# A hybrid attention and SSD block on one core: a softplus series on another engine, one joined run of half matmuls, filler matmuls, and a new order

## The chip, the core and the metric

The kernel runs on one core of a Trainium2 chip. The core has five engines that work side by side, each with its own in-order queue of instructions: PE (TensorE, matrix products; its weight loads are shown apart as PEld), DVE (VectorE), ACT (ScalarE), POOL (GpSimd) and SP (SyncE, which issues DMAs here). Data lie in SBUF; PE writes to PSUM, which has eight banks. The metric is the device time of one execution in microseconds, the median of several executions. Before the change it is 804.33 us (three runs: 802.57, 804.33, 809.08).

## What is computed

The input `x` holds 32 sequences of 256 tokens with 128 features, f32. Four sublayers follow, each as `x = x + f(layernorm(x))`:

```python
x = x + attn_a(layernorm(x))     # gated delta rule: a scan over time, done in blocks
x = x + ffn(layernorm(x))        # silu(x wg) * (x wu) wd, hidden size 384
x = x + attn_b(layernorm(x))     # SSD (a state space layer): 4 heads of 64, chunks of 32
x = x + ffn(layernorm(x))        # the same weights
```

The change lies in `attn_b`. Its core:

```python
xBC = silu(causal_conv4(xBC))                 # x, B, C
dt = softplus(dt + dt_bias)                   # one number per token and head
dA_cs = cumsum(dt * A)                        # within a chunk
y_diag = (C B^T * exp(dA_cs_i - dA_cs_j), lower triangle) @ (x * dt)
y_off = exp(dA_cs) * (C @ carried state)
y = (y_diag + y_off + x * D) * silu(z)
out = (y * rsqrt(mean(y*y) + eps) * norm_w) @ W_out
```

## The kernel before

Two sequences (512 tokens, four tiles of 128) make a unit; there are 16 units, each going through all four sublayers. The kernel does not issue instructions as it builds them. `units()` records every operation of all units in a `Planner` (`pl`): its engine, an assumed busy time, an assumed latency, what it reads and writes. Then `run()` writes one order for the whole program. It takes, again and again, the operation that can start first; among those within 20 ns of it, the one with the smallest key. The key is the unit's nominal time (`at`: 17.9 us per unit plus the unit's entry of `SHIFT`; `LAST` shortens the distance of the last units) plus how far the operation is from the end of its unit's longest path. `HOP` is the time that a result is assumed to need to another engine, `SLACK` the time before a buffer can be used again. `SWITCH` is the handicap of an ACT operation that needs another function table, `KEEP` that of a PE operation that changes between full and half tile (`cut`), and `CUT` the time which that change is assumed to take. Operations given to `batch` are placed directly one after another on PE. At the end the operations are emitted in order of planned start, so each engine's queue is fixed when the program is built; on the chip, semaphores hold each instruction until its inputs are there.

PSUM is handed out in eight slots (kind "ps"); a planned buffer is bound to a bank when its first operation is placed.

The parts that the change touches:

- In `ssd`, lines 1010 to 1033: `z` is dt before the softplus, [128 x 16] for a unit. softplus(z) = max(z, 0) + log(1 + e), with e = exp(-|z|), made on ACT. The log is a series: p = 1/(2 + e), r = 2 e p, then a polynomial in r squared by five steps, times r. All of it runs on DVE (`vec`): two instructions for p, one for r, one for the square, one for the first term, five for the polynomial, one for the product with r, one for `dt`. Then POOL makes `dA = dt * A`.
- What follows from `dA`: `pe` and `ee` (PE, ACT), `grid` (three DVE instructions), `cs` (PE), `cut` (four DVE instructions), and six DMAs on SP (three `cuts`, one `sums_s`, two `sums_t`). `dt` itself is read by `xd` (POOL) and `f0` (DVE).
- Lines 1097 to 1178, a loop over the unit's two sequences. For each: transposes of x, `xd`, the products C B^T (`cb_ps`), the decays (`pl` on PE, Exp on ACT, `sm` on DVE), then `py` (shown as sy_ps_s in the profile): 16 products for y_diag as one batch, each two instructions, all with 64 columns of weights; then y, the carried part (`pf`, `yo`), the gate `gz`, the mean square, and the output projection (`so`).
- `power_half` on POOL (two instructions) gives every 1/sqrt: four layer norms per unit (`rstd`) and the SSD's own (`rs`).
- In the profile, L238 is `matmul`, L251 `transpose`, L259 and L261 ACT operations, L275 `vec`, L292 `pool`, L302 a DMA issue. Names end in the sublayer: _a attention, _f first FFN, _s SSD, _h second FFN.

Of the kernel before, what the change touches and what calls it, by code (L numbers as in the profile page):

```python
# [15 lines left out]
ALU = mybir.AluOpType  # L16
AX = mybir.AxisListType

P = 128
# [128 lines left out]
class Planner:  # L148
# [2 lines left out]


    SLOTS = {"ps": 8, "m": 56, "l": 10, "t": 12, "s": 64, "d": 6, "g": 6, "b": 3, "e": 4}
    SWITCH = 76800.0
    HOP, SLACK = 30.0, 130.0
    STAGE = (0.0, -8900.0, 1900.0, 0.0)
    EARLY = 0.0
    SPARE = {"ps": 0.5, "m": 3, "l": 0.5, "t": 1, "s": 2, "d": 0.5, "g": 0.5, "b": 0.5, "e": 0.5}
    LAST = 0.12
    SHIFT = (18900.0, -4200.0, 0.0, 0.0, 1500.0, 11400.0, 1600.0, 1500.0, 0.0, 0.0, 19300.0, -27800.0, -1400.0, -9200.0, -7200.0, -5400.0)  # L160
    HALF = "be"
    RATE = 270.0
    LANES = 8
    CUT = 150.0
    KEEP = 3900.0
    SIZES = {"ps": 512, "m": 512, "l": 1024, "t": 64, "s": 32, "d": 512, "g": 8192, "b": 384, "e": 12288}

    def __init__(self, tc, pools, period, window):
# [34 lines left out]
    def add(self, eng, busy, late, emit, outs, ins, table=None, after=(), lock=False):  # L203
        op = Op()
        op.eng, op.busy, op.late, op.emit, op.table, op.lock = eng, busy, late, emit, table, lock
        op.unit, op.n, op.stage = self.unit, len(self.ops), self.stage
        op.preds, op.succs, op.bufs = {p.n: p for p in after}, [], []
        op.moves, op.cut, op.batch = 0.0, 0, ()
        for v, write in [(v, False) for v in ins] + [(v, True) for v in outs]:
            if not isinstance(v, View):  # L210
                continue
            bits = v.bits()
            for other, obits, lanes, owrite in v.buf.seen:
                if (
                    other is not op and (write or owrite) and bits & obits
                    and lanes[0] < v.lanes[1] and v.lanes[0] < lanes[1]
                ):
                    op.preds[other.n] = other
            kept = v.buf.kind == "c" and not v.buf.again
            assert self.setup or not (kept and write)  # L220
            if self.setup or not kept:
                v.buf.seen.append((op, bits, v.lanes, write))
            if v.buf.kind == "c" and v.buf.tile is None:
                v.buf.tile = self.pools["c"].tile(list(v.buf.dims), v.buf.dtype, tag=v.buf.name, name=v.buf.name)
            if v.buf.kind != "c" and v.buf not in op.bufs:
                op.bufs.append(v.buf)
        for p in op.preds.values():
            p.succs.append(op)
        self.ops.append(op)
        return op  # L230


    def matmul(self, out, lhsT, rhs, start, stop, passes=2, cost=None):
        cols, n = _count(lhsT), _count(rhs)
        busy = passes * (max(2 * n, 2 * cols) / 2.4 + 4.5) if cost is None else cost

        def emit():
            self.tc.nc.tensor.matmul(real(out), lhsT=real(lhsT), rhs=real(rhs), start=start, stop=stop)  # L238


        b = out.buf
        after = [op for op, _, _, write in b.seen if write] if b.sums or not (start and stop) else []
        b.sums |= not (start and stop)
        op = self.add("PE", busy, 165, emit, [out], [lhsT, rhs], after=after)

        op.cut = 0 if cols > P // 2 else 1
        return op
# [25 lines left out]
    def vec(self, name, out, *args, ins=(), more=0, n=None, rate=0.96, **kw):  # L273
        def emit():
            getattr(self.tc.nc.vector, name)(real(out), *map(real, args), **{k: real(v) for k, v in kw.items()})  # L275

        busy = (_count(out) if n is None else n) / rate + 65 + more

        data = {"tensor_tensor": 2, "tensor_tensor_scan": 2, "scalar_tensor_tensor": 3, "tensor_scalar": 1}.get(name, 0)
        data = [v for i, v in enumerate(args[:data]) if (name, i) != ("scalar_tensor_tensor", 1)]  # L280
        lock = bool(data) and not any(isinstance(v, View) and v.buf.kind == "ps" for v in data)
        self.add("DVE", busy, 85, emit, [out], list(args) + list(kw.values()) + list(ins), lock=lock)

    def pool(self, name, out, *args, ins=(), cost=None, **kw):
        n = _count(out)
        if cost is None:
            cost = {
                "tensor_tensor": 1.66 * n + 149, "tensor_scalar": n + 260, "tensor_copy": n + 190, "memset": 0.97 * n + 60,
            }.get(name, n / 2 + 100)

        def emit():
            getattr(self.tc.nc.gpsimd, name)(real(out), *map(real, args), **{k: real(v) for k, v in kw.items()})  # L292

        lock = name == "tensor_tensor" and n > NT
        self.add("POOL", cost, 40, emit, [out], list(args) + list(kw.values()) + list(ins), lock=lock)
# [16 lines left out]
    def gates(self):  # L312
# [7 lines left out]
        for b, ops in users.items():  # L320
# [4 lines left out]
                    of.add(self.ops[n])  # L325
            b.gate = {p for op in ops for p in op.preds.values()} - of

    def at(self, unit):

        late = max(0, unit - (self.units - 3))  # L330
        return (unit - late + late * self.LAST) * self.period + self.SHIFT[unit]

    def run(self):
# [18 lines left out]
        free = dict.fromkeys(engines, 0.0)  # L352
# [9 lines left out]
        order = []  # L362
        while len(order) < len(ops):
# [39 lines left out]
            t, op = best  # L403
# [35 lines left out]
                oldest += 1  # L439
        self.span = max(op.done for op in ops)  # L440
        order.sort(key=lambda op: (op.start, op.n))
        with self.tc.manual_schedule():
            for op in order:
                for b in op.bufs:
                    if b.tile is None:
                        size = self.SIZES[b.kind]
                        flat = self.pools[b.kind].tile([1 if b.kind in "dge" else P, size], BF16 if b.kind in self.HALF else F32, tag=f"{b.kind}{b.slot[1]}", name=b.name + self.mark)
                        b.tile = flat[:, : b.size]
                        if len(b.dims) > 2:
                            names = " ".join(f"d{i}" for i in range(1, len(b.dims)))  # L450
                            b.tile = b.tile.rearrange(
                                f"p ({names}) -> p {names}", **{f"d{i}": b.dims[i] for i in range(2, len(b.dims))}
                            )
                op.emit()


# [5 lines left out]
def hybrid_block(ctx: ExitStack, tc: tile.TileContext, ins: dict, out: bass.AP):  # L462
# [24 lines left out]
    HD = d_in // NH  # L487
# [11 lines left out]
    pl = Planner(tc, pools, period=17900.0, window=6)  # L499
    vec, pool, act, copy, matmul = pl.vec, pl.pool, pl.act, pl.copy, pl.matmul  # L500
# [5 lines left out]
            pattern=pattern, channel_multiplier=by,  # L506
        )

    ident = pl.const([P, P], "ident")
    pool("memset", ident, 0.0)  # L510
    select(ident, ALU.not_equal, 0, [[-1, P]], 1, fill=1.0)

# [18 lines left out]
    for d in LEVELS:  # L531
        nb = P // (2 * d)
        m = pl.const([P, nb, d], f"m_{d}")
# [471 lines left out]
    def ssd(g, x):  # L1005
        n = f"s{g}"
# [3 lines left out]
        z = small_([P, NT, NH], f"z_{n}")  # L1010
# [6 lines left out]
        sp = small_([P, NT, NH], f"sp_{n}")  # L1017
# [3 lines left out]
        r, p = small_([P, NT, NH], f"r_{n}"), small_([P, NT, NH], f"p_{n}")  # L1021
        vec("tensor_scalar", p, sp, 2.0, None, ALU.add)
        vec("reciprocal", p, p, more=110)
        vec("scalar_tensor_tensor", r, sp, 2.0, p, ALU.mult, ALU.mult)
        vec("tensor_tensor", sp, r, r, ALU.mult)
        vec("tensor_scalar", p, sp, 1.0 / (13 * 4**6), None, ALU.mult)
        for k in range(5, 0, -1):
            vec("scalar_tensor_tensor", p, p, 1.0 / ((2 * k + 1) * 4**k), sp, ALU.add, ALU.mult)
        vec("scalar_tensor_tensor", sp, p, 1.0, r, ALU.add, ALU.mult)
        dt = small_([P, NT, NH], f"dt_{n}")  # L1030
        vec("scalar_tensor_tensor", dt, z, 0.0, sp, ALU.max, ALU.add)
        dA = small_([P, NT, NH], f"dA_{n}")
        pool("tensor_tensor", dA, dt, bc(neg_a, NT), ALU.mult, cost=295)

# [11 lines left out]
        a, b = (grid[:, i, :, :].via(lambda v: v.rearrange("p h j -> p j h")) for i in range(2))  # L1046
# [31 lines left out]
        for b in range(NB):  # L1078
# [3 lines left out]
            y = big([P, SEQS, 2 * P], f"cy_{n}_{b}")  # L1082
# [11 lines left out]

        x3 = big([P, NT, P], f"x3_{g}")
        d4 = d_skip[:, None, :, None].to_broadcast([P, 2, NH, HD])
        for s in range(SEQS):
            js = slice(2 * s, 2 * s + 2)

# [5 lines left out]
            xd = big([P, 2, NH, HD], f"xd_{n}_{s}")  # L1105
            xe = big([P, NH, HD], f"xe_{n}_{s}")
# [15 lines left out]
            for c in range(2):  # L1122
# [7 lines left out]
                if c == 0:  # L1130
# [6 lines left out]
                )  # L1137
                ms.append(m)

            pl.batch([  # L1140
                matmul(
                    py[:, c, h * HD : (h + 1) * HD].part(to), m[:, h, to], xd[:, c, h, :], True, True, cost=62,
                )
                for c, m in enumerate(ms) for h in range(NH) for to in (slice(0, P // 2), slice(P // 2, P))
            ])
            vec("tensor_tensor", y, py, y, ALU.add)
            pf = bank([P, NH, HD], f"pf_{n}_{s}")
            matmul(pf, bc_[:, 2, :], xe, True, True)
# [96 lines left out]
```

## Time and profile before

| | us |
|---|---|
| median of three runs | 804.33 |
| the profiled execution | 806.73 |
| its span, first to last instruction | 804.9 |
| PE, idle time within the span | 60.2 |
| DVE, idle | 120.6 |
| ACT, idle | 207.7 |
| POOL, idle | 440.9 |

The page of the profile gives the busy time of each engine, and the chain of work that ended last, followed back from the last instruction. A group is all instructions with one line, engine, operation and set of tiles; its row gives the number of instructions, the busy time, the mean duration in ns, and the idle time of the engine before them with what ended it. The granted clock is the share of full speed at which PE was allowed to run; over the span its mean is 0.975. The 66 loads of ACT function tables take 1283 ns each.

The busy times in stretches (first columns), with the granted clock:

| stretch, us | PE | DVE | ACT | POOL | clock |
|---|---|---|---|---|---|
| 0 to 20 | 10.58 | 9.48 | 10.23 | 16.98 | 1.00 |
| 20 to 40 | 19.57 | 15.08 | 17.93 | 19.27 | 1.00 |
| 40 to 60 | 11.45 | 17.93 | 6.80 | 18.51 | 0.74 |
| 60 to 80 | 16.43 | 8.95 | 6.19 | 9.74 | 0.66 |
| 420 to 440 | 20.00 | 20.00 | 14.78 | 4.09 | 1.00 |
| 720 to 740 | 17.66 | 19.57 | 17.13 | 7.56 | 0.91 |
| 760 to 780 | 16.87 | 16.01 | 15.20 | 12.50 | 0.91 |

### The profile page before, as it was taken

The numbers are of one execution on the slowest core, as the hardware profiler recorded it, in microseconds if no ns is written. First come the engines' busy times: TensorE is split into PE (matmuls) and PEld (weight loads), VectorE is DVE, ScalarE is ACT, GpSimd is POOL, SyncE is SP. The second block draws the span as 40 slices with busy tenths as digits, with TensorE's granted clock in tenths as the row PEclk, the third lists the DMA queues.
The fourth block names the chain that finished last, engine by engine and source line by source line (L and its number), as shares of the span: only waits on it lengthen the run. The fifth ranks groups of instructions, "written<-read, shape, count | busy, mean of one in ns | idle before, by whom it ended". The sixth has DMA issues, their size and how long they took to land.

```text
span 804.9 us, 16786 instructions
## 1 busy us (share of the span) xinstructions
PE 744.7 (93%) x5485; PEld 616.5 (77%) x5485; DVE 684.3 (85%) x2386; ACT 597.2 (74%) x1443; POOL 364.0 (45%) x597
## 2 busy tenths in 40 slices
PE   5958999899999999999999999899999999998886
PEld 4646886687878888877988878686789988776775
DVE  4794799989988889889999689989898778999964
ACT  5833467979687877779787798897955578997862
POOL 8994332262452815514732634646631123243550
PEclk9976999999999999999999999999999999999999
DMA  5221110010110002101011002011201000000001
GB/s 145 82 68 42 29 42 1 5 33 1 56 30 24 22 7 67 42 27 33 18 30 31 27 15 58 16 45 44 67 4 43 14 5 1 5 15 5 13 10 44
DMA packets 42159, 25.48 MB, mean 32 GB/s; under 512 B 18448, under 2 KB 37840, under 8 KB 42064
## 3 DMA queue, kind: packets, MB, share of 16 engines
q1 hardware_dynamic: 41056, 24.13, 11.1%
q8 instruction: 45, 0.74, 0.4%
q14 instruction: 50, 0.41, 0.2%
q10 hardware_dynamic: 1008, 0.20, 0.1%
HBM read 19.16 MB, written 5.14 MB: 30 GB/s over the span
## 4 chain that ended last, share of the span: by engine, by line
PE 52%; DVE 20%; ACT 15%; POOL 5%; issue 3%; DMA 2%; SPq 1%; ACTq 0%; DVEq 0%; POOLq 0%
PE p_a L238 6%; PE fy_f L238 5%; DVE cy_s L275 4%; PE fy_h L238 4%; PE fg_f L238 3%; ACT L261 3%; PE sy_ps_s L238 3%; PE so_s L238 2%; PE fu_f L238 2%; PE pc_s L238 2%; PE fg_h L238 2%; PE fu_h L238 2%; PE pt_a L251 2%; DVE u_a L275 2%; PE cb_ps_s L238 2%
## 5 line engine op out<-in xcount | busy, mean ns | idle before, releaser
L275 DVE SCALAR_TENSOR_TENSOR cy_s<-pc_s,cw,cy_s 128x510 f32<-128x510 f32 (+2 forms) x192 | 137.6, 731 | 2.9 <-ACT cy_s L261 2.3
L261 ACT ACT_TABLE_LOAD x66 | 84.7, 1283 | 9.9 <-DMA x<-in_L_attn_a_x_dram 5.8
L238 PE MATMUL fy_f<-wdT,hT_f 128*128 128x128 f32 x384 | 74.5, 280 | 0.0
L238 PE MATMUL fy_h<-wdT,hT_h 128*128 128x128 f32 x384 | 72.1, 281 | 0.6 <-DVE hT_h L275 0.3
L238 PEld LDWEIGHTS fy_f<-wdT,hT_f 128*128 128x128 f32 x384 | 61.4, 191 | 6.3 <-issue 3.6
L238 PE MATMUL pc_s<-xT_s,w_xbc 128*128 128x512 f32 x128 | 64.5, 599 | 1.3 <-ACT gT_s L259 0.7
L238 PEld LDWEIGHTS fy_h<-wdT,hT_h 128*128 128x128 f32 x384 | 59.1, 191 | 8.1 <-issue 4.3
L275 DVE TENSOR_TENSOR step_a<-rows_a,u_a 128x16 f32<-128x16 f32 (+14 forms) x240 | 51.7, 216 | 7.5 <-DMA rows_a<-blocks_a 3.1
L275 DVE TENSOR_TENSOR u_a<-u_a,step_a 128x16 f32<-128x16 f32 (+14 forms) x240 | 54.3, 227 | 3.9
L261 ACT ACTIVATE cy_s<-pc_s,cb,cw 128x512 f32<-128x512 f32 x64 | 48.3, 779 | 9.3 <-PE pc_s L238 9.1
L292 POOL TENSOR_TENSOR xd_s<-xt_s,dt_s 128x512 f32<-128x512 f32 x32 | 33.2, 1045 | 42.9 <-ACT xt_s L259 42.2
L238 PE MATMUL so_s<-w_out,gT_s 128*128 128x128 f32 x256 | 45.8, 290 | 1.9 <-DVE cy_s L275 1.2
L238 PEld LDWEIGHTS so_s<-w_out,gT_s 128*128 128x128 f32 x256 | 39.7, 204 | 6.6 <-ACT cy_s L261 1.4
L261 ACT ACTIVATE sc_s<-cy_s 128x512 f32<-128x512 f32 x64 | 38.9, 636 | 3.6 <-DVE cy_s L275 1.9
L275 DVE SCALAR_TENSOR_TENSOR sm_s<-pl_s,cb_s 128x512 f32<-128x512 f32 x64 | 41.3, 680 | 0.3 <-ACT pl_s L261 0.2
L292 POOL TENSOR_TENSOR sy_s<-sy_s,yo_s 128x256 f32<-128x256 f32 x32 | 24.6, 773 | 35.5 <-DVE sy_s L275 14.2
L238 PEld LDWEIGHTS p_a<-t_a,neg_a 128*128 128x128 f32 x256 | 36.4, 203 | 5.5 <-ACT t_a L259 3.7
L238 PE MATMUL p_a<-t_a,neg_a 128*128 128x64 f32 x256 | 38.1, 280 | 1.8 <-DVE x L275 1.3
L238 PEld LDWEIGHTS p_a<-x_a,t_a 128*128 128x128 f32 x256 | 36.6, 201 | 3.7 <-ACT t_a L259 2.3
L238 PE MATMUL p_a<-x_a,t_a 128*128 128x64 f32 x256 | 37.9, 274 | 1.0 <-ACT t_a L259 1.0
L259 ACT COPY t_a<-pt_a 128x256 f32<-128x256 f32 (+1 forms) x64 | 20.2, 316 | 24.0 <-PE pt_a L251 22.9
L275 DVE TENSOR_TENSOR hT_f<-fth_f,fu_f 128x512 f32<-128x512 f32 x48 | 31.2, 681 | 7.3 <-PE fu_f L238 4.8
(253 smaller groups left out, 2420.7 us busy)
## 6 DMA issues: line engine op xcount, KB each, us to landing
rows_a<-blocks_a SPq DMA_DIRECT2D x128, 64.0 KB
x<-in_L_attn_a_x_dram SPq DMA_DIRECT2D x16, 256.0 KB
dec_a<-row_a SPq DMA_DIRECT2D x16, 256.0 KB
out_dram<-x SPq DMA_DIRECT2D x16, 256.0 KB
blocks_a<-neg_a SPq DMA_DIRECT2D x128, 4.0 KB
cuts_s<-cut_s SPq DMA_DIRECT2D x48, 8.0 KB
sums_t<-cuts_s SPq DMA_DIRECT2D x32, 12.0 KB
sums_s<-cuts_s SPq DMA_DIRECT2D x16, 24.0 KB
```

The lines of the kernel that those rows point to most:

```text
L238: self.tc.nc.tensor.matmul(real(out), lhsT=real(lhsT), rhs=real(rhs), start=start, stop=stop)
L251: self.tc.nc.tensor.transpose(real(out), real(in_), real(ident))
L259: self.tc.nc.scalar.copy(real(out), real(in_))
L261: self.tc.nc.scalar.activation(real(out), real(in_), func, bias=real(bias), scale=real(scale), **kw)
L275: getattr(self.tc.nc.vector, name)(real(out), *map(real, args), **{k: real(v) for k, v in kw.items()})
L292: getattr(self.tc.nc.gpsimd, name)(real(out), *map(real, args), **{k: real(v) for k, v in kw.items()})
```

## The change

Four things, all in one version.

The ten DVE instructions of the series from r on go to POOL. [...]each fused step becomes a tensor_scalar in place and a tensor_tensor (`tiny`); the square and the first term stay single instructions. The two instructions for p stay on DVE.

The products of `py` are gathered over both sequences and placed as one batch of 32; what follows them moves into a second loop over the sequences.

After the order is made, `keep_busy` goes through PE's operations. Before one that is the first to write its bank, where the plan leaves PE idle for more than 300 ns, it notes a number of filler products: 70% of the idle time over 223 ns, so many whole products. They multiply the identity matrix by itself into the bank that the operation is about to overwrite.

The planner's constants are changed, so the order of the whole program is another.

```diff
-    SWITCH = 76800.0
-    HOP, SLACK = 30.0, 130.0
+    SWITCH = 46100.0
+    HOP, SLACK = 70.0, 230.0
     STAGE = (0.0, -8900.0, 1900.0, 0.0)
...
-    LAST = 0.12
-    SHIFT = (18900.0, -4200.0, 0.0, 0.0, 1500.0, 11400.0, 1600.0, 1500.0, 0.0, 0.0, 19300.0, -27800.0, -1400.0, -9200.0, -7200.0, -5400.0)
+    LAST = 0.11
+    SHIFT = (18900.0, -4200.0, -4300.0, -3500.0, -2500.0, 11400.0, 1600.0, 1500.0, 0.0, 0.0, 13600.0, -22200.0, -1400.0, -9200.0, -7200.0, -5400.0)
...
     CUT = 150.0
-    KEEP = 3900.0
+    IDLE, WARM = 300.0, 0.7
+    KEEP = 2500.0
...
+    def keep_busy(self, order):
+        written, free = set(), 1700.0
+        for op in order:
+            if op.eng != "PE":
+                continue
+            bank = next(b for b in op.bufs if b.kind == "ps")
+            gap = op.start - free
+            if gap > self.IDLE and bank not in written and not op.cut:
+                op.warm, op.bank = int(gap * self.WARM / 223), bank
+            written.add(bank)
+            free = op.start + op.busy
...
         order.sort(key=lambda op: (op.start, op.n))
+        self.keep_busy(order)
...
+                for _ in range(op.warm):
+                    n = min(P, op.bank.size)
+                    one = self.ident.real()
+                    self.tc.nc.tensor.matmul(op.bank.flat[:, :n], lhsT=one, rhs=one[:, :n], start=True, stop=True)
                 op.emit()
...
         vec("tensor_scalar", p, sp, 2.0, None, ALU.add)
         vec("reciprocal", p, p, more=110)
-        vec("scalar_tensor_tensor", r, sp, 2.0, p, ALU.mult, ALU.mult)
-        vec("tensor_tensor", sp, r, r, ALU.mult)
-        vec("tensor_scalar", p, sp, 1.0 / (13 * 4**6), None, ALU.mult)
+
+        def tiny(out, in_, scalar, other, op0, op1):
+            pool("tensor_scalar", in_, in_, scalar, None, op0, cost=227)
+            pool("tensor_tensor", out, in_, other, op1, cost=290)
+
+        tiny(r, sp, 2.0, p, ALU.mult, ALU.mult)
+        pool("tensor_tensor", sp, r, r, ALU.mult, cost=290)
+        pool("tensor_scalar", p, sp, 1.0 / (13 * 4**6), None, ALU.mult, cost=250)
         for k in range(5, 0, -1):
-            vec("scalar_tensor_tensor", p, p, 1.0 / ((2 * k + 1) * 4**k), sp, ALU.add, ALU.mult)
-        vec("scalar_tensor_tensor", sp, p, 1.0, r, ALU.add, ALU.mult)
+            tiny(p, p, 1.0 / ((2 * k + 1) * 4**k), sp, ALU.add, ALU.mult)
+        tiny(sp, p, 1.0, r, ALU.add, ALU.mult)
         dt = small_([P, NT, NH], f"dt_{n}")
-        vec("scalar_tensor_tensor", dt, z, 0.0, sp, ALU.max, ALU.add)
+        tiny(dt, z, 0.0, sp, ALU.max, ALU.add)
...
+        halves, held = [], []
         for s in range(SEQS):
...
-            pl.batch([
-                matmul(
-                    py[:, c, h * HD : (h + 1) * HD].part(to), m[:, h, to], xd[:, c, h, :], True, True, cost=62,
-                )
+            halves += [
+                (py[:, c, h * HD : (h + 1) * HD].part(to), m[:, h, to], xd[:, c, h, :])
                 for c, m in enumerate(ms) for h in range(NH) for to in (slice(0, P // 2), slice(P // 2, P))
-            ])
+            ]
+            held.append((y, py, bc_, xe))
+        pl.batch([matmul(*half, True, True, cost=62) for half in halves])
+        for s, (y, py, bc_, xe) in enumerate(held):
             vec("tensor_tensor", y, py, y, ALU.add)
```

More of the change, by code (lines that the diff above doesn't have):

```diff
@@ L207, in add @@
         op.preds, op.succs, op.bufs = {p.n: p for p in after}, [], []
-        op.moves, op.cut, op.batch = 0.0, 0, ()
+        op.moves, op.cut, op.batch, op.warm = 0.0, 0, (), 0
         for v, write in [(v, False) for v in ins] + [(v, True) for v in outs]:
@@ L447, in run @@
                         flat = self.pools[b.kind].tile([1 if b.kind in "dge" else P, size], BF16 if b.kind in self.HALF else F32, tag=f"{b.kind}{b.slot[1]}", name=b.name + self.mark)
-                        b.tile = flat[:, : b.size]
+                        b.flat = b.tile = flat[:, : b.size]
                         if len(b.dims) > 2:
@@ L507, in select @@
         )
-    ident = pl.const([P, P], "ident")
+    ident = pl.ident = pl.const([P, P], "ident")
     pool("memset", ident, 0.0)
```

## The prediction

> **What bounds the kernel now.** I read the page first: the busy times, then the shares of the chain that ended last. After that came the same sums cut into stretches of time, the timeline at the places that stood out, and the groups of what the change touches. The profiled execution took 806.7 us (span 804.9 and 1.8 around it), 2.4 above the median of 804.3. My sum is made against 806.7, and 2.4 is taken off at the end.
>
> ```profile
> PE 744.7 (93%) x5485; PEld 616.5 (77%) x5485; DVE 684.3 (85%) x2386; ACT 597.2 (74%) x1443; POOL 364.0 (45%) x597
> ...
> PE 52%; DVE 20%; ACT 15%; POOL 5%; issue 3%; DMA 2%; SPq 1%; ACTq 0%; DVEq 0%; POOLq 0%
> ```
> PE leads, in busy time and on the chain; DVE is second. POOL has room: 441 us idle. Next, stretches (width, busy time per engine, then the granted clock of PE as the first bare number):
>
> ```profile
> 48.00:58.00 10.00, 6.08 (x20) 4.82 (x21) 9.70 (x28) 2.82 (x6) 9.88 (x16) 0.50 0.21 68
> 58.00:65.00 7.00, 5.13 (x24) 3.01 (x22) 6.79 (x25) 2.52 (x12) 2.21 (x8) 0.99 0.02 3
> 65.00:78.00 13.00, 11.70 (x51) 10.67 (x52) 4.12 (x16) 3.09 (x9) 8.53 (x11) 0.50 0.23 64
> 100.00:740.00 640.00, 614.49 (x4598) 510.28 (x4598) 573.35 (x2021) 507.91 (x1202) 267.86 (x419) 0.99 0.10 26
> 740.00:805.00 65.00, 53.05 (x477) 44.33 (x475) 44.76 (x114) 40.28 (x88) 24.71 (x36) 0.93 0.08 21
> ```
> From 100 to 740 us PE is busy for 614 of 640, so only 25.5 us are visibly idle there. At the start it works at half clock for about 23 us, in two pieces. After 740 the clock is 0.93 and PE idles 12 us of 65. The PE timeline of the start:
>
> ```profile
> 47.31 0.66 PE L251 MATMUL kT_ps_a<-ident,k_a 128*128 128x128 f32 x4 [4.48 <-POOL k_a L292]
> 51.25 1.63 PE L251 MATMUL xT_ps_a<-ident,xn_a 128*128 128x128 f32 x4 [3.28 <-ACT xn_a L261]
> ...
> 62.62 0.67 PE L238 MATMUL pvq_a<-xT_a,gT_a 128*128 128x256 f32 x2 [0.92 <-DVE neg_a L275]
> ...
> 64.96 1.97 PE L238 MATMUL p_a<-t_a,neg_a 128*128 128x64 f32 x8 [0.55 <-ACT t_a L259]
> ...
> 83.36 1.04 PE L238 MATMUL p_a<-t_a,neg_a 128*128 128x64 f32 x8
> ```
> Eight matmuls of one kind take 1.97 us at half clock and 1.04 at full.
>
> **Part 1, filled stretches.** Where the written order leaves PE idle for over 300 ns before a matmul that opens a bank, 70% of that gap is filled with 128x128 products of `ident`. One costs 0.22 us: two instructions, and back-to-back ones of this shape start 0.11 us apart (so_s, p_a at full clock). What it can bring at the start: the chain from 65 to 78.6 us consists of 12.2 us of PE pieces (1.98, 1.99, 1.11, 1.86, 1.97, 1.71, 1.58). At full clock these shrink by 1 - 1.04/1.97 = 0.47, which is 5.7 us. The earlier half-clock piece brings nothing, because DVE (9.70 of 10) and POOL (9.88) hold that stretch. Here rule and row differ. The row says that half clock began at 65 us behind gaps of only 0.92, 0.41 and 0.55 us. The Trainium skill (TensorE: Matmul & The Clock Gate, "HAM oscillation") asks for no idle gap over about 3.4 us. By the rule only the gaps of 4.48 and 3.28 need a fill, and those lie where PE is not the limit: gain 0. By the row, sparse work is enough to lose the clock, and filling the short gaps too is worth up to 5.7. I follow the row but expect the fill to miss some of it: 4 us. From 720 to 780 the clock was 0.91 in each 20 us row, (1 - 0.91) x 60 / 0.5 = 11 us at half; PE has about a third of the chain there, and half of 11 x 0.37 is 2: I take 1.5. The price: the filler stands in PE's queue whether the gap arrives or not. Against 60 us of idle PE, some 45 of them after the first matmul, 70% is about 31 us or 140 products (an estimate). Those that meet a busy PE cost their full 0.22 us. Both ends for the whole part: -8 and +16.
>
> **Part 2, softplus series to GpSimd.** Per unit ten DVE instructions go, 160 in all: five of the form below, and r_s, two sp_s, one of the two tensor_scalar on p_s, and dt_s.
>
> ```profile
> L275 DVE SCALAR_TENSOR_TENSOR p_s<-p_s,sp_s 128x16 f32<-128x16 f32 x80 | 13.5, 172 | 0.5
> L292 POOL TENSOR_TENSOR dA_s<-dt_s,neg_a 128x16 f32<-128x16 f32 x16 | 3.5, 216 | 58.4 <-DVE dt_s L275 51.0 <-DVE f_s L275 3.7 <-DVE sp_s L275 3.5
> L292 POOL TENSOR_SCALAR rs_s<-rs_s 128x2 f32<-128x2 f32 x32 | 8.8, 275 | 23.7 <-ACT sy_s L261 21.9
> ```
> Their groups hold 13.5 + 3.7 + 2.7 + 2.6 + 2.8 + 3.2 = 28.5 us of DVE. On POOL each fused step becomes two: nine tensor_scalar and nine tensor_tensor per unit. A tensor_tensor of this very shape takes 216 ns; from a tensor_scalar to the tensor_tensor that needs it, starts lie 275 ns apart, so about 75 ns are added to a dependent step. That gives 9 x 0.28 + 9 x 0.29 = 5.1 us per unit, 82 us in all, some 70 of it busy: POOL goes to about 435 us, 54%. The rule speaks against it: the Trainium skill (GPSIMD Engine Reference, "Engine selection") says that elementwise work belongs on VectorE and costs about 2x on GpSimd. The rows say 5.1 against 1.8, nearly 3x, so worse. By the rule alone the part loses; but what matters is which queue it sits in. On DVE the ten steps are spread between other work: from the end of the Exp to the end of dt the 16 units need 2.6 to 13.3 us, median 9.9. On POOL I expect one or two DVE steps and then 5 us. The first user is dA_s on POOL, then grid on DVE, cs on PE, cut on DVE and six DMAs on SP. POOL waits 51.0 us in all for dt_s today, and the next xd_s comes 2.6 to 24 us after dA_s, so a somewhat later dt is covered, and an earlier one moves SP's six issues and the loads queued behind them forward. If that cover goes, each microsecond of delay costs one.
>
> What it is worth: pieces of these tiles on the chain are p_s 4.7, sp_s 1.2, dt_s 1.1, r_s 0.4 = 7.4 us, of which a fifth (the two steps that stay) remains: 6. DVE's 20% of the chain times 28.5 gives 5.7, the same. Against that stands the lock of the two engines:
>
> ```profile
> 130.53 0.25 DVE L275 RECIPROCAL p_s<-p_s 128x16 f32<-128x16 f32 x1
> 130.81 1.22 DVE L275 SCALAR_TENSOR_TENSOR r_s<-sp_s,p_s 128x16 f32<-128x16 f32 x1
> ...
> 130.74 1.26 POOL L292 TENSOR_TENSOR x_a<-u_a,blk 128x512 f32<-128x512 f32 x1 [0.75 <-issue]
> ```
> A 165 ns step took 1.22 us, exactly under a POOL tensor_tensor. The change adds 144 tensor_tensor of 0.216 us, 31 us of such cover. DVE runs instructions with two SBUF inputs about a fifth of the time (u_a and step_a 106 us, e_a 36, gz_s 21), so some 6 us of stall, 1.2 on the chain. I take a gain of 4.5; ends +9 gain and 6 loss.
>
> **Part 3, one run of half matmuls for both sequences.** The 64-column products of sy_ps run at 23 to 31 ns each, but the first starts 205 ns behind an ordinary matmul instead of 111, and the next ordinary one 151 ns after the last. A run thus costs 0.21 us. Today there are 22 runs, since the order pairs many by itself; 16 would remain: 1.3 us. Sequence 0's y, norm and projection wait for sequence 1, a few us, hidden by other units in mid-run; in the last unit both sat in one run already (64 half matmuls at 757 us), so the tail pays nothing. I take 1; ends 1.3 gain and 5 loss.
>
> **Part 4, the order.** Units 2, 3 and 4 are due 3.5 to 4.3 us earlier, units 10 and 11 move by -5.7 and +5.6. The planner reckons 40 ns more per hop between engines and 100 ns more before a slot is free. A table switch is held back less: 66 loads of 1.28 us now, and ten more would put 13 us on an ACT with 208 us free, about 2 us at its 15% of the chain. An order cannot be costed from this trace. Its gain is bounded by the 25.5 us of idle PE in mid-run and the 12 after 740; a loss by about one wait of 1 us per unit, 16. Larger assumed latencies should put dependent steps further apart, which is what a PE with hundreds of short waits lacks. I take a gain of 5, ends 14 and -16.
>
> **The sum.** 4 + 1.5 + 4.5 + 1 + 5 = 16 us off 806.7 is 790.7; less 2.4, 788.
>
> **Rivals.** A, slower: POOL's queue becomes the limit. The series is 18 dependent instructions, 5.1 us in one strict queue. A rstd behind it (0.28 + 1.03 us) waits 2.5 us on average; norm, transposes and PE wait for that. If it comes on the chain in every unit, 16 x 2.5 = 40 us are lost against the 16 gained: about 828. It decides from 1 us per unit on. For it: every norm passes POOL, four per unit. Against: POOL is idle over half the time, most of its waits are for DVE, and the order interleaves. B, nothing: the fill meets gaps that are not there. 140 products are 31 us of PE; half of them on a busy PE is 16 us, which takes back the rest: 800 to 808. C, larger gain: with DVE relieved in the rows where it is full (19.6 of 20 at 720 to 740), the mid-run waits go too, half of 25.5 us: about 775.
>
> **How the numbers follow.** About 8 us either way is what a measurement can tell from no change. Likeliest case, 776 to 796: 0.45; C, below 776: 0.17; B and its like, within 1%: 0.16; A and a worse order: 0.22. So faster 0.62, same 0.16, slower 0.22. The range, 768 to 822, leaves out the far ends of C and A.
>
> **What would show it.** Right: PE clock near 1.0 between 65 and 78 us; a few hundred more PE instructions; DVE busy near 660, POOL near 435; dt within 7 us of its Exp; 16 runs of half matmuls. Wrong: POOL above 8% of the chain, rstd waiting behind p_s on POOL; PE busy up by 25 us with the span unchanged; more waits of PE for xn or x_a than now.

## The result, and the profile after

The changed kernel takes 812.95 us against 805.61 for the kernel before, both medians of six runs. The ratio estimated from the runs is 1.0102, with an interval of 1.0075 to 1.0129 (the plain quotient of the two medians is 1.0091): about 1% slower, where 788 us, about 2% faster, was forecast. The time lies inside the stated range of 768 to 822, but on the other side of no change. The profiled execution took 812.5 us, with a span of 810.7.

The busy times, and the chain that ended last, of the changed kernel:

```profile
PE 757.8 (93%) x5805; PEld 640.3 (79%) x5805; DVE 678.6 (84%) x2226; ACT 593.2 (73%) x1439; POOL 430.1 (53%) x885
...
PE 47%; DVE 26%; ACT 14%; POOL 4%; issue 4%; SPq 2%; DMA 1%; DVEq 0%; ACTq 0%; POOLq 0%
```

PE has 320 instructions more: 160 filler products, some 35 us of PE at 0.22 us each (an estimate). Busy PE rose by 13 us against before, and by 23 against the same order without fillers (734.6 in e1, below). POOL is where it was forecast (435), DVE is not: 160 instructions left it, and its busy time fell by 5.7 us, not 28.5. On the chain PE gave up five points and DVE took six.

The 28.5 us were too many from the start. They are a sum of durations, and on DVE the records of neighbouring instructions overlap: all durations of the kernel before add up to 833 us, its busy time is 684. DVE's timeline in the kernel before:

```profile
133.80 0.16 DVE L275 TENSOR_TENSOR sp_s<-r_s 128x16 f32<-128x16 f32 x1
133.88 0.74 DVE L275 SCALAR_TENSOR_TENSOR cy_s<-pc_s,cw,cy_s 128x510 f32<-128x510 f32 x1
```

The step on sp_s is recorded with 0.16 us, but the next instruction starts 0.08 us after it. What the 160 steps really free is seen in e4 below, where they leave DVE and everything else keeps its place: 13.7 us of busy time.

The same stretches as before (width, busy times of PE, PEld, DVE, ACT and POOL, then the granted clock):

```profile
48.00:58.00 10.00, 6.71 (x51) 5.74 (x51) 9.66 (x33) 2.27 (x6) 9.72 (x14) 0.94 0.28 81
58.00:65.00 7.00, 6.54 (x37) 5.24 (x36) 6.28 (x25) 3.28 (x13) 4.01 (x9) 0.84 0.11 38
65.00:78.00 13.00, 11.51 (x89) 10.46 (x89) 9.99 (x36) 4.43 (x15) 6.29 (x12) 1.00 0.00 1
100.00:740.00 640.00, 609.46 (x4671) 515.04 (x4669) 550.52 (x1833) 494.11 (x1177) 330.35 (x702) 1.00 0.10 26
740.00:811.00 71.00, 60.74 (x557) 51.58 (x557) 51.45 (x127) 44.39 (x99) 26.60 (x39) 0.98 0.07 20
```

The clock is where it was meant to be: 1.00 from 65 to 78 us, where it was 0.50, and 0.994 over the span against 0.975. From 65 to 78 us PE ran 89 instructions where it had run 51. But this trace cannot credit the fillers with it. That of the changed kernel without them (e1, the fastest of its six runs) reads nearly the same there, and its first unit is as far: the first xn_f (the norm before an FFN) starts at 93.2 us in both. The line of e1:

```profile
65.00:78.00 13.00, 11.85 (x90) 10.40 (x89) 10.00 (x36) 4.37 (x15) 6.30 (x12) 1.00 0.01 1
```

From 100 to 740 us PE is busy for 5 us less than before, although fillers lie in that stretch: there the loss shows.

PE's timeline at the start of the changed kernel; L473 is the filler:

```profile
50.01 4.18 PE L473 MATMUL xT_ps_a<-ident 128*128 128x128 f32 x36
56.57 1.63 PE L252 MATMUL xT_ps_a<-ident,xn_a 128*128 128x128 f32 x4 [2.38 <-ACT xn_a L262]
...
67.59 1.08 PE L239 MATMUL p_a<-t_a,neg_a 128*128 128x64 f32 x8
```

Eighteen fillers stand before the transposes that wait for xn_a, and 2.38 us of waiting are left behind them. The eight p_a matmuls, 1.97 us before, now take 1.08, and 1.08 in e1 too. In mid-run the fillers mostly stand behind a wait instead of in it:

```profile
693.43 1.83 PE L473 MATMUL fg_h<-ident 128*128 128x128 f32 x14 [2.08 <-DVE xr_h L276]
695.01 0.48 PE L239 MATMUL fg_h<-xT_h,wgT 128*128 128x512 f32 x1
```

The input of a filler is the constant `ident`, so what it waits for here can only be the bank that it writes. PE stands idle for 2.08 us until the bank is free, then runs seven fillers (14 instructions), and only then fg_h. Between 100 and 740 us there are 29 such groups with 70 fillers: PE idles 16.0 us before them and 0.5 us behind them.

The series on POOL (instructions, busy us, mean ns, idle time before):

```profile
L293 POOL TENSOR_SCALAR p_s<-p_s 128x16 f32<-128x16 f32 x96 | 24.5, 256 | 7.6
L293 POOL TENSOR_TENSOR p_s<-p_s,sp_s 128x16 f32<-128x16 f32 x80 | 17.8, 223 | 4.7
```

Its 288 instructions sum to 70 us, as forecast. The forecast of an early `dt` fell: from the end of the Exp to the end of `dt` the 16 units need 6.9 to 19.3 us, median 10.3, no less than on DVE (9.8, counted in the same way). The steps do not run as one block on POOL either; the order puts other work between them.

### The profile page after: what moved, and what is told of

The parts are those of the page before. It is cut to its first block, busy times and chain, and to the rows that moved or that the text cites. A ratio compares the mean times of both kernels' runs of the same rounds, so it can differ in the third digit from the quotient of the medians.

```text
span 810.7 us, 17572 instructions
## 1 busy us (share of the span) xinstructions
PE 757.8 (93%) x5805; PEld 640.3 (79%) x5805; DVE 678.6 (84%) x2226; ACT 593.2 (73%) x1439; POOL 430.1 (53%) x885
## 4 chain that ended last, share of the span: by engine, by line
PE 47%; DVE 26%; ACT 14%; POOL 4%; issue 4%; SPq 2%; DMA 1%; DVEq 0%; ACTq 0%; POOLq 0%
DVE cy_s L276 6%; PE p_a L239 5%; PE fy_f L239 4%; PE fy_h L239 3%; PE fu_f L239 3%; DVE u_a L276 2%; PE so_s L239 2%; ACT L262 2%; PE fu_h L239 2%; PE fg_h L239 2%; DVE sm_s L276 2%; DVE step_a L276 2%; PE po_a L239 2%; PE fg_f L239 2%; PE pt_a L252 2%
## 5 line engine op out<-in xcount | busy, mean ns | idle before, releaser
L276 DVE TENSOR_TENSOR step_a<-rows_a,u_a 128x48 f32<-128x48 f32 (+14 forms) x240 | 56.6, 238 | 8.6 <-DMA rows_a<-blocks_a 5.0
L276 DVE TENSOR_TENSOR u_a<-u_a,step_a 128x60 f32<-128x60 f32 (+14 forms) x240 | 54.0, 227 | 3.3
L293 POOL TENSOR_TENSOR sy_s<-sy_s,yo_s 128x256 f32<-128x256 f32 x32 | 27.2, 854 | 34.5 <-DVE sy_s L276 29.1
L239 PE MATMUL so_s<-w_out,gT_s 128*128 128x128 f32 x256 | 43.8, 280 | 0.0
L239 PEld LDWEIGHTS so_s<-w_out,gT_s 128*128 128x128 f32 x256 | 37.4, 192 | 4.7 <-issue 1.9
L276 DVE TENSOR_TENSOR_SCAN e_a<-dec_a,s_a 128x256 f32<-128x256 f32 (+1 forms) x64 | 38.5, 626 | 0.0
L262 ACT ACTIVATE pl_s<-pl_s 128x512 f32<-128x512 f32 x64 | 33.9, 582 | 5.7 <-DVE grid L276 3.1
L239 PE MATMUL po_a<-pr_a,k_a 128*128 128x128 f32 x192 | 37.2, 278 | 0.3 <-DVE pr_a L276 0.3
L252 PE MATMUL pt_a<-ident,x_a 128*128 128x128 f32 x192 | 33.6, 280 | 4.0 <-DVE x_a L276 3.0
```

The source lines that it names most:

```text
L252: self.tc.nc.tensor.transpose(real(out), real(in_), real(ident))
L262: self.tc.nc.scalar.activation(real(out), real(in_), func, bias=real(bias), scale=real(scale), **kw)
```

## The experiments

The theories are numbered as in the expectations. Theory 1: the changed constants make a worse order. Theory 2: the fillers cost (2b: in mid-run only; 2c: the old order swallows any lead). Theory 3: the series on POOL costs. Theory 4: the joined run costs. Theory 5, which came up after the first four runs: the order that the kernel before has is picked out of many, and any fresh order is worse, whatever caused it. Theory 6: the code changes are worth something once this luck is taken out. Each ratio is to the kernel before on the same chip.

**Fillers alone, with every queue's order kept.** The order is made before the fillers are put in, so taking them out or putting them in moves nothing else. e1 takes them out of the changed kernel, e3 puts them into the kernel before.

```diff
# e1, the changed kernel
         order.sort(key=lambda op: (op.start, op.n))
-        self.keep_busy(order)
# e3, the kernel before: IDLE, WARM, keep_busy and the fillers of the changed kernel
+        self.keep_busy(order)
```

> The changed kernel without its filler matmuls; every queue keeps its order, 320 PE instructions fewer. Theory 1 (the written order is what costs): the clock falls back to about 0.975 and the time rises from 1.010 of before to 1.012 to 1.018. Theory 2 (fillers run where the gap did not come and push real work back): the time falls to 1.000 to 1.005. If neither, within 0.2% of 1.010: the clock gain at the start and the fillers' own time cancel, or both are hidden.

Measured: 1.0104 (1.0065 to 1.0144), the same as with fillers, though the clock fell from 0.989 to 0.994 over the six runs to 0.965 to 0.977 (0.977 in the profiled one). Theory 2 falls for the changed kernel, and so does theory 1's "slower without". What is left is the third possibility: the clock that the fillers gain and the PE time that they take cancel, or both are hidden.

> The kernel before with fillers only; its order is kept in every queue. Prediction's sum: 0.7% faster (5.5 us: 0.993), with the clock at 0.99 and above. Theory 2: 0.3 to 1% slower.

Measured: 1.0037 (1.0014 to 1.0060), 2.6 us slower, clock 0.987. The stretches of the start in e3:

```profile
48.00:58.00 10.00, 9.77 (x58) 8.61 (x58) 9.81 (x26) 2.92 (x6) 9.88 (x16) 0.86 0.22 59
58.00:65.00 7.00, 4.10 (x15) 2.32 (x13) 6.76 (x25) 2.68 (x13) 2.22 (x7) 0.71 0.03 3
65.00:78.00 13.00, 12.62 (x78) 11.36 (x77) 3.79 (x17) 3.83 (x12) 7.65 (x10) 0.76 0.24 63
```

The clock from 65 to 78 us rises from 0.50 to 0.76, not to 1. Between 58 and 65 us one gap is left, and half clock begins at 61.0 us, within it:

```profile
61.71 1.19 PE L239 MATMUL pvq_a<-xT_a,gT_a 128*128 128x256 f32 x2 [2.88 <-DVE neg_a L276]
```

What the fillers gave is read from the first xn_f of some units, a norm in each unit's second sublayer (us from the start of the span):

| unit | before | e3 | e9 |
|---|---|---|---|
| 1 | 99.6 | 96.4 | 95.5 |
| 4 | 187.4 | 185.7 | 184.2 |
| 8 | 369.9 | 369.8 | 365.9 |
| 12 | 576.8 | 577.9 | 572.8 |
| 16 | 678.5 | 679.8 | 674.6 |

In this trace the lead of 3.2 us is there at the start, gone by 370 us, and 1.3 us behind at the end. Each column is one execution, and executions of one kernel differ by as much: 117 runs of the kernel before, on five chips, range from 801 to 812 us, those with a clock of 0.98 and more at 803.3 on average (54 runs), those with 0.973 and less at 809.1 (24 runs). Next, e9: fillers at the start only.

```diff
-            if gap > self.IDLE and bank not in written and not op.cut:
+            if gap > self.IDLE and op.start < 90000 and bank not in written and not op.cut:
```

> The kernel before, order kept, with fillers only where the plan is before 90 us. The filled kernel e3 was 3.2 to 3.7 us ahead of the kernel before at 100 to 220 us and behind it by 1.2 us at 577 us. Theory 2b (fillers win at the start and cost in mid-run): the lead stays, 3 to 4 us faster, 0.995 to 0.997. Theory 2c (mid-run takes back any lead, because the order was made for the old start): 0.999 to 1.002.

Measured: 0.9988 (0.9965 to 1.0012). In the profiled execution the lead of about 4 us stays to the last unit (799 us), but that was the lowest of its runs; the median is 802.9 against 805.4. The clock of that execution was 0.989, that of the profiled kernel before 0.975, so part of the 4 us can be the luck of the draw. In time, a gain from the fillers at the start is not clear of nothing. That those in mid-run cost something in this order is likelier: the intervals of e3 and e9 do not meet (1.0014 to 1.0060, 0.9965 to 1.0012). The same edit on the changed program (e18, on the kernel of e12 below):

> The kernel of e12 (changed, HOP 75, 1.0056), order kept, with fillers only where the plan is before 90 us. Theory 2b (fillers in mid-run cost 0.3 to 0.5%): 1.000 to 1.003. If mid-run fillers are free: 1.005 to 1.007.

Measured: 1.0052 (1.0033 to 1.0071), where e12 has 1.0056. Fillers in mid-run cost nothing that shows there, so 2b does not hold for that order.

**The series, moved between the engines at the same places of the order.** In e2 the changed kernel's order stays, but each pair of POOL steps is issued as one fused step on DVE. In e4 the order of the kernel before stays, and each DVE step is issued as the POOL pair.

```diff
# e2 (shortened), in tiny(), after the two pool(...) lines: planned for POOL, issued on DVE; the two single steps likewise
+            pl.ops[-2].emit = lambda: None
+            pl.ops[-1].emit = lambda: nc.vector.scalar_tensor_tensor(out, in_, scalar, other, op0, op1)
# e4 (shortened), for each fused vec(...) of the series: planned for DVE, issued on POOL; the two single steps likewise
+            nc.gpsimd.tensor_scalar(in_, in_, scalar, None, op0)
+            nc.gpsimd.tensor_tensor(out, in_, other, op1)
```

> The changed kernel with the softplus series issued on DVE again, fused as before, but at the very places of the written order; fillers and all other queues as in the changed kernel. Theory 3 (the series on POOL costs: lock of DVE by 144 tensor_tensor, and the queue of POOL): 0.4 to 1% faster than the changed kernel, 1.000 to 1.006 of before, and DVE's other instructions get shorter by about 15 us in all. Theory 1 (order): DVE gains 28 us of work and the time is the same or longer, 1.010 to 1.016.

Measured: 1.0245 (1.0199 to 1.0290), 1.4% slower than the changed kernel. DVE's busy time went from 678.6 to 700.2, while its idle time stayed (132.1 and 132.5 us):

```profile
PE 770.9 (93%) x5805; PEld 650.4 (78%) x5805; DVE 700.2 (84%) x2386; ACT 593.2 (71%) x1439; POOL 365.0 (44%) x597
```

(This trace is that of the slowest of the six runs, 834.4 us; their median is 825.6.) The other DVE instructions did not get shorter: step_a, u_a and e_a together were busy 151.0 us against 149.1. Theory 3 falls for the changed order.

> The kernel before with the softplus series issued on POOL, at the places that the order has for the DVE steps; all else keeps its place. Prediction: up to 0.6% faster if DVE's relief counts (0.994). Theory 3: 0.3 to 1.2% slower, as the steps now stand in POOL's queue ahead of the rstd and xd work, and DVE's instructions with two SBUF inputs get longer by 10 to 20 us in all.

Measured: 1.0307 (1.0266 to 1.0348), slower than theory 3 said, but not by its lock. step_a, u_a and e_a were busy 141.7 us, against 142.4 before, and the durations of all DVE instructions outside the series add up to 2.3 us more, on grid alone 2.5.

```profile
PE 750.9 (91%) x5485; PEld 622.1 (75%) x5485; DVE 670.6 (81%) x2226; ACT 597.0 (72%) x1443; POOL 432.4 (52%) x885
```

DVE is busy for 13.7 us less than before, but idle for 157 us instead of 120.6. Most of that is one wait, in DVE's waits of e4 (total, times, longest):

```profile
DVE grid L275 <- POOL dA_s L292: 23.1, 8, 5.2
```

In the kernel before the same row reads:

```profile
DVE grid L275 <- POOL dA_s L292: 0.7, 2, 0.3
```

DVE stands still eight times, up to 5.2 us, because grid is queued where dA was due with the series on DVE. POOL's share of the chain doubled from 5 to 10%. This is rival A's kind of loss, in DVE's queue instead of behind a rstd.

e17 plans the series for DVE and keeps everything else of the changed kernel.

```diff
-        tiny(r, sp, 2.0, p, ALU.mult, ALU.mult)
+        vec("scalar_tensor_tensor", r, sp, 2.0, p, ALU.mult, ALU.mult)
...
```

> The changed kernel with the softplus series on DVE, planned there (fresh order, changed constants, joined run and fillers kept). If the series on POOL carries the gain of the changed program in fresh orders: 1.018 to 1.03 of before. If it carries none: 1.003 to 1.015.

Measured: 1.0306 (1.0272 to 1.0340). Two kernels, one with the order kept and one with it made anew, put the series on DVE 1.4 and 2.0% behind the changed kernel. Neither is a clean measure: the order of e2 was made for the series on POOL, as that of e4 was for DVE, and e17 is a single fresh order, where fresh orders of one program differ by as much (below).

**The constants alone.**

```diff
-    SWITCH = 76800.0
-    HOP, SLACK = 30.0, 130.0
+    SWITCH = 46100.0
+    HOP, SLACK = 70.0, 230.0
...
```

and likewise `LAST`, `SHIFT` and `KEEP`.

> The kernel before with the changed constants of the planner alone (another order of the same instructions). Theory 1 (the constants make the worse order): 1.010 to 1.020 of before. Theory 4 (the joined run costs): 0.995 to 1.003, as the constants are not to blame. Theory 5 (any fresh order is about 1% worse than the one that before has): 1.005 to 1.02 as well, and then e7 is no better than the changed kernel.

Measured: 1.0288 (1.0231 to 1.0344), 23 us slower with exactly the same instructions. Busy times and chain of e5:

```profile
PE 748.4 (91%) x5485; PEld 615.4 (74%) x5485; DVE 691.9 (84%) x2386; ACT 597.5 (72%) x1445; POOL 364.9 (44%) x597
...
PE 43%; DVE 25%; ACT 19%; POOL 4%; issue 3%; DMA 3%; SPq 2%; DVEq 0%; ACTq 0%
```

PE does the same work in about the same busy time (748 against 745), but it idles for 826.0 - 748.4 = 77.6 us of the span, where it had idled for 60.2. The share of PE on the chain falls by nine points, and DVE and ACT take them. DVE is also busy 7.6 us longer with the same instructions; step_a alone rose from 51.7 to 57.1. So this part of what kept DVE's busy time up in the changed kernel came with the constants, not with the series.

e7 is the reverse, the changed code with the old constants.

> The changed kernel with the constants of before: series on POOL, joined run, fillers, planned anew. Theory 1: faster than the changed kernel, 0.995 to 1.003 of before. Theory 4: as slow as the changed kernel or slower, 1.01 to 1.025. Theory 5: 1.01 to 1.03, since the constants were made for another program.

Measured: 1.0195 (1.0137 to 1.0253). The old constants are no better for the changed program, so theory 1 as stated falls: neither set is good or bad by itself. With the changed code the new constants are even ahead, 1.0102 against 1.0195.

**The joined run, in and out.** e6 adds it to the kernel before, e8 takes it out of the changed one, both planned anew.

```diff
# e6; e8 is the reverse
-            pl.batch([matmul(...) for c, m in enumerate(ms) for h in range(NH) for to in ...])
+            halves += [...]
+        pl.batch([matmul(*half, True, True, cost=62) for half in halves])
```

> The kernel before with the half matmuls of both sequences in one run, old constants, planned anew. Prediction: 1.3 us for six fewer changes of tile form, 0.998. Theory 4 (sequence 0's output held up by sequence 1, and DVE's work in larger lumps): 1.008 to 1.02. Theory 5: 1.005 to 1.02, whatever the joined run itself does.

> The changed kernel with the half matmuls of each sequence in their own run again, new constants, planned anew. Theory 4: 0.5 to 1.5% faster than the changed kernel, 0.995 to 1.005 of before. Theory 1: 1.008 to 1.02. Theory 5: 1.01 to 1.03.

Measured: 1.0244 (1.0192 to 1.0295) for e6, 1.0239 (1.0174 to 1.0304) for e8. The edit in one direction cost 2.4%, and in the other 1.4% against the changed kernel. Theory 4 would have them move apart; that both lose is what theory 5 says.

**Changes that mean nothing.** e10 moves the nominal time of unit 8 by +0.1 us, e13 by -0.1 us; e11 raises `HOP` by 5 ns.

```diff
# e10: the ninth entry of SHIFT (unit 8, counted from 0); e13: -100.0
-    SHIFT = (..., 1600.0, 1500.0, 0.0, 0.0, 19300.0, ...)
+    SHIFT = (..., 1600.0, 1500.0, 100.0, 0.0, 19300.0, ...)
# e11
-    HOP, SLACK = 30.0, 130.0
+    HOP, SLACK = 35.0, 130.0
```

> The kernel before with one entry of SHIFT (unit 8) 0.1 us later: a change that means nothing, but another order from there on. Theory 5 (the order before has is picked out of many; any fresh one is worse): 1.008 to 1.03. Theory 1 or 4 (the named parts are to blame): 0.997 to 1.004.

> The kernel before with HOP 35 in place of 30: 5 ns more per hop in the plan, another order nearly everywhere. Theory 5: 1.01 to 1.03. Theory 1 or 4: 0.997 to 1.004.

> The kernel before with the entry of SHIFT for unit 8 0.1 us earlier. If its order is a picked one: 1.008 to 1.03, as e10 and e11. If e10 and e11 were bad luck: 0.997 to 1.006.

Measured: e10 1.0140 (1.0092 to 1.0187), e11 1.0344 (1.0301 to 1.0388), e13 1.0073 (1.0050 to 1.0095). Theory 5 is shown for the order of the kernel before: a tenth of a microsecond in the plan costs 6 to 11 us on the chip, whichever way it goes. Busy times and chain of e10:

```profile
PE 747.5 (92%) x5485; PEld 613.3 (75%) x5485; DVE 687.0 (84%) x2386; ACT 595.9 (73%) x1443; POOL 361.2 (44%) x597
...
PE 40%; DVE 29%; ACT 14%; POOL 7%; issue 4%; SPq 3%; DMA 3%; DVEq 0%; POOLq 0%; ACTq 0%
```

The signature is like that of e5: nearly the same busy PE, more idle PE (815.8 - 747.5 = 68.3 us), and a chain that runs less through PE and more through DVE and the DMA queue. The first xn_f of the ninth unit starts at 413.0 us, as before (412.7); the tenth at 473.0 instead of 464.1; the last at 698.6 instead of 678.5.

**Fresh orders of both programs.** To see whether the code changes are worth anything beside this, small steps of the same kind were taken from the changed constants: with the changed code (e12, e14, e15) and, as the pair of e12, without it (e16).

```diff
# e12 and e16 75.0; e14 80.0
-    HOP, SLACK = 70.0, 230.0
+    HOP, SLACK = 75.0, 230.0
# e15: as in e10, on the changed kernel
-    SHIFT = (..., 1600.0, 1500.0, 0.0, 0.0, 13600.0, ...)
+    SHIFT = (..., 1600.0, 1500.0, 100.0, 0.0, 13600.0, ...)
```

> The changed kernel with HOP 75 in place of 70. If the changed kernel's constants were picked for its own program (theory 5): 1.015 to 1.035 of before, slower than the changed kernel. If it has no picked order: spread around it, 1.005 to 1.016.

> The changed kernel with HOP 80. Theory 6 (the code changes are worth about 1.3% in a fresh order, 1.026 down to 1.012 on the mean of three each): 1.003 to 1.02. One spread for both programs: 1.015 to 1.035.

> The changed kernel with the entry of SHIFT for unit 8 0.1 us later, the same step as in e10. Theory 6: 1.003 to 1.02. One spread: 1.015 to 1.035.

> The kernel before with the changed constants and HOP 75, the pair of e12 without its code changes. Theory 6: 1.018 to 1.035. One spread: 1.003 to 1.02.

Measured: e12 1.0056 (1.0034 to 1.0077), e14 1.0078 (1.0042 to 1.0115), e15 1.0121 (1.0072 to 1.0171), e16 1.0206 (1.0156 to 1.0255).

| fresh orders | ratios to the kernel before | mean |
|---|---|---|
| old code (e5, e10, e11, e13, e16) | 1.0288, 1.0140, 1.0344, 1.0073, 1.0206 | 1.021 |
| changed code (the change itself, e7, e12, e14, e15) | 1.0102, 1.0195, 1.0056, 1.0078, 1.0121 | 1.011 |

With the same constants the changed code is ahead twice: 1.0288 to 1.0102 and 1.0206 to 1.0056, by 1.5 to 1.8%. Over all ten orders the means differ by 1.0%, but the two sets overlap, and with five orders each (spreads of 1.1 and 0.5%) that difference is not beyond chance. e6, e8 and e17 (1.0244, 1.0239 and 1.0306), which have a part of the code changes, are in neither row. Theory 6 is likely, not shown. That the changed kernel's own order is a picked one is not borne out: two of its three neighbours have lower ratios.

## Why the prediction was wrong

The step that failed is part 4, "the order": a gain of 5 us was taken, with ends of 14 gained and 16 lost. Its own measure is e5, the constants with nothing else: 23 us lost, beyond the far end of 16. The reason given, that larger assumed latencies put dependent steps further apart, may hold for the planner; on the chip it was not the size of `HOP` that counted. HOP 35 lost 28 us with the old constants, and HOP 75 with the changed code did better than HOP 70. The old order was not one of many like it. All five of the old program's fresh orders are slower than it, by 0.7 to 3.4%, so replacing it costs about 2% on the mean of the five, 17 us. And it is not the constants alone that replace it: the series on POOL and the joined run make the planner decide anew as well, which parts 2 and 3 put at nothing. With the old constants kept, the changed code still lost 2% (e7). The trace of before had the sign of this: PE visibly idle for only 25.5 us out of 640, with four other engines in between. I read that as a bound on the gain. It was also the thing at risk: with the constants alone PE idled 17 us more over the span (77.6 against 60.2).

Part 1, fillers: in the old order the mechanism is right at the start. The clock from 65 to 78 us rose to 0.76 (e3), and leads of 3 to 4 us are in the single traces of e3 and e9 against 4 forecast. That the changed kernel had 1.00 there, and p_a at full clock, is a sign that came true by luck, as far as the traces go: its new order has both without any filler in the trace of e1, which left the fillers no slow stretch there to mend. The price was named but the sum left it out: in mid-run the fillers stand behind the wait for their bank, and in the trace of e3 a lead of 3.2 us turned into 1.3 behind. As a whole the part was put at a gain of 5.5; it measures 2.6 us lost in the old order and nothing in the changed one. Between rule and row, e3 speaks for the row: half clock began in a gap of 2.88 us, shorter than the two that the prediction filled by the rule.

Part 2, the series: perhaps right in sign, with wrong terms. Forecast was a gain of 4.5 us; e2 and e17 put the series on DVE 1.4 and 2.0% (12 and 16 us) behind, each with the reservation made there. The relief of DVE was mis-sized: 28.5 us is the sum of durations that overlap, and at kept places 13.7 us leave DVE (e4), or 21.6 come back to it (e2). That this relief carries the gain is likely, as DVE's idle time in e2 stayed, but it was not isolated. The lock, put at 6 us of stall, does not appear in e4. Wrong was that `dt` would come early (10.3 us against 9.8), and that a later one is covered. e4 shows what the cover is worth: it holds only where the order knows when dA comes. The prediction's "nearly 3x" sets two instructions against one: a single tensor_tensor takes 223 ns on POOL, a fused step 172 on DVE, and each fused step became two, which makes 4.4 us of POOL out of 1.8 of DVE per unit. The rule of the Trainium skill (GPSIMD Engine Reference, "Engine selection"), which gives about 2x for instructions with two inputs only, is not refuted by this (1.3x for one instruction of this size); if it paid to set it aside, the likely reason is that DVE had less time to spare than POOL.

Part 3, the joined run: the count is right (22 runs of half matmuls became 16); the 1.3 us cannot be seen beside the changes of order that the edit brings.

So 1% slower can be read as about 23 us lost by the new constants' order (e5) and about 15 regained by the three code changes with the same constants (1.0288 down to 1.0102), against 11 forecast for them. The split depends on the way taken: code first loses 16 us (e7), and the constants then regain 7.5. On both ways the first step off the old order is the one that loses. Of the rivals, A had the sign, but its mechanism, a rstd behind the series in POOL's queue, is not what happened: POOL's share of the chain fell from 5 to 4%, and of the 64 rstd only 12 stand directly behind a step of the series, 11 of which start within 0.6 us of their input and one 2.3 us after it. What stays open is which of the orders' many waits makes the old order good; no single one was found, and no experiment isolated one.

## What to carry to other kernels

When a program's order is written out by a planner and is better than its neighbours, every edit that makes the planner decide anew first loses that lead; here it was 0.7 to 3.4%. (How the old order was found is not on record; its sixteen uneven entries of `SHIFT` look like a choice made by trying.) So before judging an edit, move something that means nothing and see what that costs, and judge the edit by several orders with and without it, or at kept places of the order. Little visible idle time on the leading engine is not only a small room for gain: it can also mean that a fresh order has something to lose.

## What the runs showed of the hardware

Half clock does not need a long gap, and the sum of the gaps does not tell it either. In the kernel before, half clock began at 65 us behind gaps of 0.92, 0.41 and 0.55 us, all after 61.7 us. In the changed kernel a single gap of 1.89 us, as long as those three together, ended at 66.4 us, and the clock stayed at 1.00 from 65 to 78. In e3 it was one gap of 2.88 us, from 58.8 to 61.7 us, and half clock from 61.0 to 71.3.

Within one kernel a higher clock goes with a shorter time (803.3 and 809.1 us for the two groups of runs of the kernel before). Bought with fillers it was no gain: 0.989 to 0.994 with them and 0.965 to 0.977 without gave the same ratio (the changed kernel and e1), while they added 23 us of busy PE in the traces.

A short DVE instruction takes less of DVE than its record says: in the kernel before, cy_s started 0.08 us after a 0.16 us step on sp_s, and 160 such steps, recorded with 28.5 us, freed 13.7 us of busy time (e4).

The 144 added tensor_tensor on POOL, 0.22 us each, left DVE's step_a, u_a and e_a as long as they were (141.7 us in e4, 142.4 before), while a 1.26 us one had held a DVE step for 1.22 us in the kernel before.
